# The transient factor of the last stage as 32x32 matmuls on diagonal tiles, for four images at once

## The chip, the cores and the metric

The kernel runs on one core of one Trainium2 chip. The metric is the device time of one execution in microseconds (us); the time before is the median of three runs, 3254.34 us (3249.64 to 3259.84).

## The reference

Sixteen images of sixteen channels with 256x256 points go through two layers. Both add to their input something computed from its group norm: a 3x3 circular convolution (written with FFTs in the reference), and then a Laplace layer with complex poles.

```python
    x = x + _L0_conv_ref(_gn(x), L0_conv_weight)
    x = x + _L1_conv_ref(_gn(x), L1_conv_ty, L1_conv_tx, ...)
```

Of the Laplace layer this is what matters here:

```python
        output_residue2 = jnp.einsum('bikpq,ikpq->bkpq', D, weights_residue)
        x1 = jnp.fft.ifft2(output_residue1, s=(Ny, Nx), axes=(-2, -1)).real
        E1 = jnp.exp(weights_pole1[..., None] * tyc)
        E2 = jnp.exp(weights_pole2[..., None] * txc)
        F = jnp.einsum('kbpq,bipz->kbiqz', output_residue2, E1)
        x2 = jnp.einsum('kbiqz,biqx->kizx', F, E2).real
        return x1 + x2 / Nx / Ny
```

`x1` is the steady part, an inverse transform. `x2` is the transient part: for one image k and one output channel i it is a product of three matrices, a table of exponentials along y, the residues of the image, and a table of exponentials along x.

## The kernel before

All arithmetic is float32. A float32 matmul is shown in the profile as two instructions of TensorE, so counts there are twice those of the code. The kernel has four stages:

- the convolution, from the start to about 760 us, with an order written out by hand; tables for later stages are computed beside it, among them the exponentials (`make_exps`, L384 to L426), which go to DRAM as `eD`: `eD[0]` along y, `eD[1]` along x;
- the forward transforms (L560 to L700), at whose end the residues of all images are put into the SBUF tile `o2`;
- the mixing over channels (L703 to L920), with an order written out by hand, which leaves its spectra in DRAM as `yD`;
- the last stage (L923 to L1006), which turns them back and adds the transient part. In it the framework's scheduler decides the order of the instructions on each engine from the program text, dependences and free buffers.

The last stage loops over 16 output channels `k`, and within one over four groups of four images (`b0`), so there are 64 groups and 256 images of one channel. For a channel, SP loads `yk` (its spectra, 4 MB, two buffers). For a group, SP loads `vl` (the layer's input, two buffers), and GpSimd computes four sums and differences `u` (L960) and scales a column (L963), two buffers. Then for each image:

1. `ps_h` (L974, TensorE): residues times the table along x, one matmul of 128x128 by 256 columns; ScalarE copies it to `hs` (L982).
2. `ps_p` (L985, TensorE): four matmuls of 128 columns from `u`, the inverse transform along x; ScalarE copies it to `pt` (L987).
3. `ps_f` (L990 and L991, TensorE): two matmuls from `pt` (the inverse transform along y) and two from `hs` with the table along y, all of 256 columns, in pairs that accumulate.
4. ScalarE copies one half of `ps_f` to `q` (L993); VectorE forms sum and difference `r` (L995, L996) and folds them out to the rows of `ol` (L997, L998).

After the four images VectorE adds `vl` to `ol` in one operation (L1001), and two stores to `out_y` are issued on ScalarE's queue (L1003). Each engine takes its instructions in the order of its own queue, and a DMA that is issued on ScalarE's queue stands in that order too.

The PSUM pools are `p_p` with three buffers, `p_h` with two and `p_f` with three, eight banks in all (L931 to L933). `pt`, `hs` and `q`, `r` have three buffers each, `ol` and `vl` two.

The matrix of residues that `ps_h` uses is 128x128, but only a quarter of it is not zero: rows 32kq to 32kq+31 (kq = 0 to 3 are four groups of channels or poles) belong to 16 columns of each of the two parts. The operations at L697 write it, four for each part, each with a mask column of `cols` (20 to 23):

```python
        for kq in range(4):
            nc.vector.tensor_scalar(
                o2[:, :, ro, 16 * kq : 16 * kq + 16], ps, cols[:, 20 + kq : 21 + kq], None, ALU.mult
            )
```

At its start the stage loads both tables, 2 MB each, in one tile `et` (L934 to L936), the constants `inv`, the first `yk` and the first two `vl`.

Of the kernel before, what the change touches and what calls it, by code (L numbers as in the profile page):

```python
# [9 lines left out]
FP = mybir.dt.float32  # L10
AF = mybir.ActivationFunctionType
ALU = mybir.AluOpType
AX = mybir.AxisListType
PSUM = bass.MemoryType.PSUM
DRAM = bass.MemoryType.DRAM

B = 16
C = 16
N = 256
P = 128  # L20
# [4 lines left out]
def conv_then_laplace_kernel(ctx: ExitStack, tc: tile.TileContext, a: dict, out: bass.AP):  # L25
# [15 lines left out]
    nc = tc.nc  # L41
    x = a["x"]

    cp = ctx.enter_context(tc.tile_pool(name="const", bufs=1))
    dp = ctx.enter_context(tc.tile_pool(name="scratch", bufs=1, space=DRAM))
# [6 lines left out]
    cols = const("cols", [P, 24])  # L52
    kmask = const("kmask", [P, C])
    trig = const("trig", [P, 2, P])
    o2 = cp.tile([P, B, 2, 64], FP, name="o2", tag="o2")

    vD = [dp.tile([2, P, C, N], FP, name=f"vD{b}", tag=f"vD{b}") for b in range(B)]
    aD = dp.tile([P, 2 * C, N * B], FP, name="aD", tag="aD")
    yD = dp.tile([P, 2 * C, 4, 2, 32 * B], FP, name="yD", tag="yD")
    cD = dp.tile([P, 4, 8, N], FP, name="cD", tag="cD")  # L60
    eD = dp.tile([2, P, C, 2, P], FP, name="eD", tag="eD")


    def omega(o, k, d):
# [28 lines left out]
    p1 = ExitStack()  # L93
# [290 lines left out]
    def make_exps(which):  # L384


        pl = sw.tile([P, C, 2], FP, name="s_pl", tag="s_pl")
        nc.sync.dma_start(out=pl, in_=a[f"pole_e{which + 1}"])
        t = sw.tile([P, N], FP, name="s_t", tag="s_t")
        nc.sync.dma_start(out=t, in_=a[("ty", "tx")[which]].to_broadcast([P, N]))  # L390
        sign, phase, turns = (cols[:, 2 + 3 * which + j : 3 + 3 * which + j] for j in range(3))
        pim = sw.tile([P, C], FP, name="s_pim", tag="s_pim")
        nc.vector.tensor_scalar(pim, pl[:, :, 1], sign, None, ALU.mult)
        yield
        for q in range(8):
            th = sw.tile([P, 2, N], FP, name="s_th", tag="s_th")
            rn = sw.tile([P, 2, N], FP, name="s_rn", tag="s_rn")
            ex = sw.tile([P, 2, N], FP, name="s_ex", tag="s_ex")
            for j in range(2):
                i = 2 * q + j  # L400
                nc.vector.tensor_scalar(th[:, j], t, pim[:, i : i + 1], None, ALU.mult)
                nc.scalar.activation(ex[:, j], t, AF.Exp, scale=pl[:, i, 0:1])
            nc.vector.tensor_scalar(rn, th, 1.0 / (2 * PI), turns, ALU.mult, ALU.add)
            magic = 1.5 * 2.0**23
            nc.vector.tensor_scalar(rn, rn, magic, None, ALU.add)
            nc.vector.tensor_scalar(rn, rn, magic, None, ALU.subtract)
            yield
            c1 = 6.28125
            c2 = float(np.float32(1.93500518798828125e-3))
            c3 = 2 * np.pi - c1 - c2  # L410
            for c in (c1, c2, c3):
                nc.vector.scalar_tensor_tensor(th, rn, -float(c), th, ALU.mult, ALU.add)
            nc.vector.tensor_scalar(th, th, phase, 3.1415925, ALU.add, ALU.min)
            nc.vector.tensor_scalar(th, th, -3.1415925, None, ALU.max)
            yield
            nc.scalar.activation(th, th, AF.Sin)
            yield
            nc.gpsimd.tensor_tensor(th, th, ex, ALU.mult)
            for op, eo in ((ALU.add, 0), (ALU.subtract, 1)):
                nc.gpsimd.tensor_tensor(  # L420
                    ex[:, :, eo * P : eo * P + P], th[:, :, 0:P], th[:, :, N - 1 : P - 1 : -1], op
                )
            yield
            nc.sync.dma_start(
                out=eD[which][:, 2 * q : 2 * q + 2].rearrange("p i e t -> p i (e t)"), in_=ex
            )  # L426

    def make_c():

# [105 lines left out]
    for g in range(24 * B + 3):  # L535
        conv(g)
        b, n = divmod(g, 24)
# [22 lines left out]
    p1 = ExitStack()  # L560
    kp = p1.enter_context(tc.tile_pool(name="b_const", bufs=1))
# [18 lines left out]
    m, n = cols[:, 16:17], cols[:, 17:18]  # L580
# [87 lines left out]
    for i in range(C):  # L668
        spec = ap.tile([P, 2, N, B], FP, name="spec", tag="spec")
        psd = pd.tile([P, B, 32], FP, name="psd", tag="psd")  # L670
        for b0 in range(0, B, 4):
            vf = fold(i, b0)
            t = lines(i, b0, vf)
            columns(i, b0, t, spec, psd)
        nc.scalar.dma_start(
            out=aD[:, 2 * i : 2 * i + 2].rearrange("p r n -> p (r n)"),
            in_=spec.rearrange("p r f b -> p (r f b)"),
# [14 lines left out]
    for ro in range(2):  # L692
        ps = pd.tile([P, B, 32], FP, name="psd", tag="psd")[:, :, 0:16]
        nc.tensor.matmul(ps, lhsT=jmat[:, 0], rhs=accs[:, ro], start=True, stop=False)
        nc.tensor.matmul(ps, lhsT=jmat[:, 2 - ro], rhs=accs[:, 1 - ro], start=False, stop=True)
        for kq in range(4):
            nc.vector.tensor_scalar(  # L697
                o2[:, :, ro, 16 * kq : 16 * kq + 16], ps, cols[:, 20 + kq : 21 + kq], None, ALU.mult
            )
    p1.close()  # L700
    ptab.close()

# [2 lines left out]
    kp = p2.enter_context(tc.tile_pool(name="m_const", bufs=1))  # L705
# [22 lines left out]
    sgn, nsgn, first = mcol[:, 6:7], mcol[:, 7:8], mcol[:, 8:9]  # L728
# [162 lines left out]
    for g in range(32):  # L891
# [3 lines left out]
        for n in range(0, 8, 2):  # L895
# [7 lines left out]
            for m in (n, n + 1):  # L903
                o, src = mix(m, sg, yt)
# [18 lines left out]
    p3 = ExitStack()  # L923
    kp = p3.enter_context(tc.tile_pool(name="e_const", bufs=1))
    yp = p3.enter_context(tc.tile_pool(name="yk", bufs=2))
    up = p3.enter_context(tc.tile_pool(name="ud", bufs=2))
    hp = p3.enter_context(tc.tile_pool(name="hl", bufs=3))
    qp = p3.enter_context(tc.tile_pool(name="ql", bufs=3))
    vp = p3.enter_context(tc.tile_pool(name="vl", bufs=2))
    op = p3.enter_context(tc.tile_pool(name="ol", bufs=2))  # L930
    pp = p3.enter_context(tc.tile_pool(name="p_p", bufs=3, space=PSUM))  # L931
    ph = p3.enter_context(tc.tile_pool(name="p_h", bufs=2, space=PSUM))
    pf = p3.enter_context(tc.tile_pool(name="p_f", bufs=3, space=PSUM))  # L933
    et = kp.tile([P, 2, C, 2, P], FP, name="et", tag="et")  # L934
    for j in range(2):
        nc.sync.dma_start(out=et[:, j], in_=eD[j])  # L936
    inv = kp.tile([P, 5, P], FP, name="inv", tag="inv")
    nc.sync.dma_start(out=inv, in_=a["inv"])
    cx, sx, nsx, cosY, sinY = (inv[:, j] for j in range(5))
# [1 line left out]
    for k in range(C):  # L941
        yk = yp.tile([P, 2, 2, 4, B, 32], FP, name="yk", tag="yk")
        nc.sync.dma_start(
            out=yk.rearrange("p r h c b j -> p (r h c b j)"),
            in_=yD[:, 2 * k : 2 * k + 2].rearrange("p r c h n -> p (r c h n)"),
        )
        for b0 in range(0, B, 4):
            bs = slice(b0, b0 + 4)
            vl = vp.tile([P, 2, 4, N], FP, name="vl", tag="vl")
            for j in range(4):  # L950
                nc.sync.dma_start(
                    out=vl[:, :, j], in_=vD[b0 + j][:, :, k, :].rearrange("h y x -> y h x")
# [15 lines left out]
                ALU.mult,  # L968
            )
            ol = op.tile([P, 2, 4, N], FP, name="ol", tag="ol")  # L970
            for j in range(4):
                b = b0 + j
                ps_h = ph.tile([P, N], FP, name="ps_h", tag="ps_h")
                nc.tensor.matmul(  # L974
                    ps_h,
                    lhsT=o2[:, b].rearrange("p r m -> p (r m)"),
                    rhs=et[:, 1, k].rearrange("p e t -> p (e t)"),
                    start=True,
                    stop=True,
                )  # L980
                hs = hp.tile([P, N], FP, name="hs", tag="hs")
                nc.scalar.copy(hs, ps_h)  # L982
                ps = pp.tile([P, 4, P], FP, name="ps_p", tag="ps_p")
                for n, (at, tab) in enumerate(((0, cx), (3, sx), (1, nsx), (2, cx))):
                    nc.tensor.matmul(ps[:, at], lhsT=u[:, j, n], rhs=tab, start=True, stop=True)  # L985
                pt = hp.tile([P, 2, N], FP, name="pt", tag="pt")
                nc.scalar.copy(pt, ps.rearrange("p (e n) x -> p e (n x)", e=2))  # L987
                ps = pf.tile([P, 2, N], FP, name="ps_f", tag="ps_f")
                for e, tab in ((0, cosY), (1, sinY)):
                    nc.tensor.matmul(ps[:, e], lhsT=tab, rhs=pt[:, e], start=True, stop=False)  # L990
                    nc.tensor.matmul(ps[:, e], lhsT=et[:, 0, k, e], rhs=hs, start=False, stop=True)  # L991
                q = qp.tile([P, N], FP, name="q", tag="q")
                nc.scalar.copy(q, ps[:, 1])  # L993
                r = qp.tile([P, 2, N], FP, name="r", tag="r")
                nc.vector.tensor_tensor(r[:, 0], ps[:, 0], q, ALU.add)  # L995
                nc.vector.tensor_tensor(r[:, 1], ps[:, 0], q, ALU.subtract)  # L996
                nc.vector.tensor_tensor(ol[:, :, j, 0:P], r[:, :, 0:P], r[:, :, P:N], ALU.add)  # L997
                nc.vector.tensor_tensor(  # L998
                    ol[:, :, j, N - 1 : P - 1 : -1], r[:, :, 0:P], r[:, :, P:N], ALU.subtract
                )  # L1000
            nc.vector.tensor_tensor(ol, ol, vl, ALU.add)  # L1001
            for h in range(2):
                nc.scalar.dma_start(  # L1003
                    out=out[k, bs, h].rearrange("b y x -> y b x"), in_=ol[:, h]
# [4 lines left out]
def _constants():  # L1009

    c = {}
    j = np.arange(N)
    p = np.arange(P)
# [14 lines left out]
    k = (j + P) % N - P  # L1028
# [3 lines left out]
    cols = np.zeros((P, 24))  # L1032
    even = p % 2 == 0
    cols[:, 0], cols[:, 1] = even, ~even
    first = p < 64
    cols[:, 2] = np.where(first, 1.0, -1.0)
    cols[:, 3], cols[:, 4] = np.where(first, np.pi / 2, 0), np.where(first, 0.25, 0)
    cols[:, 5] = 1.0
# [42 lines left out]
def _laid_out(x, L0_conv_weight, L1_conv_ty, L1_conv_tx, L1_conv_weights_pole1, L1_conv_weights_pole2, L1_conv_weights_residue):  # L1081
# [36 lines left out]
    z = np.broadcast_to(z[:, None, :, :, None], (2, 2, 4, 4, 2, 4, 8, 2))  # L1118
    g["pole2_k"] = z.reshape(P, 32, 2)

    e1 = p1.transpose(0, 2, 1, 3).reshape(64, C, 2)
    g["pole_e1"] = np.concatenate([e1, e1], 0)
    g["pole_e2"] = np.repeat(p2.transpose(0, 2, 1, 3).reshape(64, C, 2), 2, 0)
    return {n: np.ascontiguousarray(v) for n, v in g.items()}

# [16 lines left out]
```

## Time and profile before

| | us |
|---|---|
| median of the runs | 3254.34 |
| the profiled execution | 3263.39 |
| its span | 3261.5 |
| busy: PE / DVE / ACT / POOL over the span | 2731.3 / 1840.4 / 1342.9 / 942.9 |
| first ps_p of the last stage starts | 2449.69 |
| last pair of ps_f starts | 3251.21 |

The profile is of one execution. Its times are microseconds from the start of the span. PE is TensorE's matmuls, PEld its weight loads, DVE VectorE, ACT ScalarE, POOL GpSimd, SP the engine that issues most of the DMAs. In the groups by line, a row gives the line of the code, the engine, the operation, the tile written and those read, the shape and how often; then the busy time, the mean duration in ns, and the idle time of the engine just before such instructions with what ended it. These are rows of the last stage, from 2460 to 3250 us:

```profile
L990 PE MATMUL ps_f<-pt,inv 128*128 128x256 f32 x1009 | 313.6, 392 | 0.3
L991 PE MATMUL ps_f<-hs,et 128*128 128x256 f32 x1010 | 300.4, 379 | 0.0
L985 PE MATMUL ps_p<-inv,u 128*128 128x128 f32 x2024 | 286.8, 275 | 0.0
L998 DVE TENSOR_TENSOR ol<-r 128x256 f32<-128x256 f32 x253 | 195.5, 773 | 0.0
L974 PE MATMUL ps_h<-et,o 128*128 128x256 f32 x502 | 150.5, 382 | 3.1 <-ACT hs L982 3.1
L987 ACT COPY pt<-ps_p 128x512 f32<-128x512 f32 x253 | 149.8, 592 | 59.7 <-PE ps_p L985 51.9
L1001 DVE TENSOR_TENSOR ol<-ol,vl 128x2048 f32<-128x2048 f32 x63 | 144.4, 2292 | 2.1
L997 DVE TENSOR_TENSOR ol<-r 128x256 f32<-128x256 f32 x253 | 144.2, 570 | 42.2 <-DMA out_y<-ol 31.7 <-issue 2.3
L982 ACT COPY hs<-ps_h 128x256 f32<-128x256 f32 x251 | 97.1, 387 | 0.2
L993 ACT COPY q<-ps_f 128x256 f32<-128x256 f32 x252 | 93.8, 372 | 426.2 <-PE ps_f L991 382.3 <-DVE r L996 21.8 <-PE ps_p L985 15.7
```

Matmuls are pipelined: the mean duration of one reaches over the start of the next, so durations of a row add up to more than its busy time. A view in order of time gives the start, the length and the instruction, where several that follow each other are put together with their number.

### The profile page before, as it was taken

How to read it: one execution, taken by the hardware profiler on the slowest of the kernel's cores; microseconds unless marked ns; L12 is line 12 of the kernel's file. 1: busy time of each engine (PE TensorE's matmuls, PEld its weight loads, DVE VectorE, ACT ScalarE, POOL GpSimd, SP SyncE). 2: the span in 40 equal slices, each digit the busy share in tenths (PEclk: the TensorE clock that was granted, in tenths of full speed). 3: DMA queues.
4: the chain of work that ended last, by engine and by line, in shares of the span. 5: the costliest groups of instructions: out<-in, count | busy, mean ns of one | idle time of the engine just before them, and what ended most of it. 6: DMA issues, size and time to landing. Idle time of an engine off the chain costs nothing.

```text
span 3261.5 us, 104676 instructions
## 1 busy us (share of the span) xinstructions
PE 2731.3 (84%) x46188; PEld 1949.9 (60%) x46188; DVE 1840.4 (56%) x3584; ACT 1342.9 (41%) x2640; POOL 942.9 (29%) x753
## 2 busy tenths in 40 slices
PE   4878787796999999996676777777749999999998
PEld 1333333344777677764444545555438998999987
DVE  5555665565555555555343333334317888788787
ACT  2454676563444444442233333333313333333333
POOL 1111111002444455442111111111105444444442
PEclk9899898898999999997799899999979999999999
DMA  5455565665445555444265555655576776767764
GB/s 215 162 187 172 200 237 195 222 222 171 173 164 203 198 194 185 167 165 182 81 175 160 158 160 163 173 163 168 166 242 231 259 259 235 281 239 252 267 223 155
DMA packets 409158, 637.89 MB, mean 196 GB/s; under 512 B 30336, under 2 KB 364544, under 8 KB 400128
## 3 DMA queue, kind: packets, MB, share of 16 engines
q1 hardware_dynamic: 338816, 496.96, 46.8%
q10 hardware_dynamic: 69888, 134.23, 10.8%
q8 instruction: 364, 5.96, 0.7%
q14 instruction: 90, 0.74, 0.1%
HBM read 353.72 MB, written 277.35 MB: 193 GB/s over the span
## 4 chain that ended last, share of the span: by engine, by line
PE 47%; issue 10%; DVE 4%; DMA 4%; POOL 1%; ACT 1%; ACTq 0%; SPq 0%; DVEq 0%; POOLq 0%
PE ps_s L791 10%; PE ps_mix L839 9%; PE ps_f L990 5%; PE ps_f L991 5%; PE ps_p L985 5%; PE ps_x L648 3%; PE ps_y L608 3%; PE ps_y L616 3%; DMA out_y<-ol 3%; PE ps_h L974 2%; DVE ol L998 1%; DVE ol L1001 1%; DVE ol L997 1%; DVE sg L902 1%; DMA vl<-vD 1%
## 5 line engine op out<-in xcount | busy, mean ns | idle before, releaser
L223 PE MATMUL ps_conv<-xt,wc 32*32 32x512 f32 x12288 | 485.6, 646 | 29.9 <-ACT vt L241 20.8
L960 POOL TENSOR_TENSOR u<-yk 128x512 f32<-128x512 f32 x256 | 340.1, 1357 | 487.9 <-PE ps_p L985 411.3
L791 PE MATMUL ps_s<-ct,w 64*32 64x256 f32 (+1 forms) x8448 | 326.9, 415 | 132.6 <-issue 69.4
L839 PE MATMUL ps_mix<-abd,sg 128*32 128x64 f32 x16384 | 297.7, 229 | 134.9 <-issue 134.5
L839 PEld LDWEIGHTS ps_mix<-abd,sg 128*32 128x32 f32 x16384 | 262.8, 116 | 209.6 <-issue 199.1
L223 PEld LDWEIGHTS ps_conv<-xt,wc 32*32 32x32 f32 x12288 | 230.9, 107 | 235.9 <-issue 144.2
L902 DVE COPY sg<-ps_s 128x512 f32<-128x512 f32 x248 | 172.4, 699 | 342.8 <-PE ps_s L791 342.7
L624 ACT ACTIVATE t<-ps_y,vmr 128x768 f32<-128x768 f32 x256 | 229.7, 900 | 261.0 <-PE ps_y L616 235.9
L767 POOL TENSOR_TENSOR w<-v,mcol 128x2048 f32<-128x2048 f32 x33 | 118.8, 3599 | 717.2 <-DVE v L764 694.1
L608 PE MATMUL ps_y<-tabE,vf 128*128 128x256 f32 x1024 | 308.5, 383 | 17.1 <-DVE vf L595 13.2
L902 ACT COPY sg<-ps_s 128x512 f32<-128x512 f32 x248 | 168.5, 681 | 371.7 <-PE ps_s L791 371.6
L990 PE MATMUL ps_f<-pt,inv 128*128 128x256 f32 x1024 | 318.7, 393 | 0.3
L985 PEld LDWEIGHTS ps_p<-inv,u 128*128 128x128 f32 x2048 | 289.5, 192 | 33.7 <-POOL u L963 14.2
L616 PE MATMUL ps_y<-tabO,vf 128*128 128x256 f32 x1024 | 306.0, 381 | 2.0 <-DVE vf L598 2.0
L791 PEld LDWEIGHTS ps_s<-ct,w 64*32 64x32 f32 x8448 | 163.6, 115 | 239.4 <-issue 113.4
L991 PE MATMUL ps_f<-hs,et 128*128 128x256 f32 x1024 | 305.0, 379 | 0.0
L985 PE MATMUL ps_p<-inv,u 128*128 128x128 f32 x2048 | 291.2, 275 | 13.5 <-POOL u L963 13.5
L993 ACT COPY q<-ps_f 128x256 f32<-128x256 f32 x256 | 95.3, 372 | 432.7 <-PE ps_f L991 388.8
L590 POOL TENSOR_TENSOR s<-vy 128x1024 f32<-128x1024 f32 x64 | 151.7, 2371 | 419.9 <-issue 289.3
L648 PE MATMUL ps_x<-t,trig 128*128 128x512 f32 x512 | 247.3, 605 | 0.0
L253 DVE BATCH_NORM_STATS2 vst<-vt 128x6 f32<-128x512 f32 x128 | 88.0, 687 | 278.1 <-ACT vt L241 278.1
L608 PEld LDWEIGHTS ps_y<-tabE,vf 128*128 128x128 f32 x1024 | 193.9, 191 | 78.9 <-issue 43.8
(197 smaller groups left out, 4162.4 us busy)
## 6 DMA issues: line engine op xcount, KB each, us to landing
xt<-in_x SPq DMA_DIRECT2D x32, 2193.0 KB, 9.4
vD<-vt SPq DMA_DIRECT2D x256, 256.0 KB, 3.1
vy<-vD SPq DMA_DIRECT2D x256, 256.0 KB, 4.2
aD<-spec ACTq DMA_DIRECT2D x16, 4096.0 KB, 14.0
abd<-aD SPq DMA_DIRECT2D x512, 128.0 KB, 3.1
yD<-yt SPq DMA_DIRECT2D x256, 256.0 KB, 4.5
yk<-yD SPq DMA_DIRECT2D x16, 4096.0 KB, 14.2
vl<-vD SPq DMA_DIRECT2D x256, 256.0 KB, 6.3
```

What stands on the lines that cost most here:

```text
L223: nc.tensor.matmul(acc[r][32 * c : 32 * c + 32], lhsT=ready[b][0][rows, phase, tap], rhs=halves[b][u // 2][rows, q : q + 5 : 4, 2 - tap : ...
L608: nc.tensor.matmul(ps[:, xo, 0:N], lhsT=vf[:, xo, 0, j], rhs=tabE[:, 0 : i + 2 : i + 1], start=True, stop=False, skip_group_check=True,)
L616: nc.tensor.matmul(ps[:, xo, P : P + N], lhsT=vf[:, xo, 1, j], rhs=tabO[:, i : C + 1 : C - i], start=False, stop=True, skip_group_check=True,)
L624: nc.scalar.activation(t[:, :, j].rearrange("p e l n -> p e (l n)"), ps[:, :, 0:384], AF.Copy, scale=vmr[:, 0, b0 + j, i : i + 1],)
L648: nc.tensor.matmul(ps[xo], lhsT=tab, rhs=t[:, xo, j : j + 2, 0:3:2], start=True, stop=True)
L791: nc.tensor.matmul(ps[odd][32 * iq : 32 * iq + 32, ro, fy], lhsT=w[rows, iq, kk, ro], rhs=ct[rows, iq, kk, fy], start=True, stop=True,)
L839: nc.tensor.matmul(ps[32 * c : 32 * c + 32, j], lhsT=sg[:, 64 * c + 8 * n + j], rhs=abd[n // 2][:, :, c, 8 * (n % 2) + j], start=True, sto ...
L902: (nc.scalar.copy, nc.vector.tensor_copy)[j % 2](o, src)
L960: nc.gpsimd.tensor_tensor(u[:, :, j].rearrange("p b (c n) -> p c b n", c=4), in0, in1, o)
L985: nc.tensor.matmul(ps[:, at], lhsT=u[:, j, n], rhs=tab, start=True, stop=True)
L990: nc.tensor.matmul(ps[:, e], lhsT=tab, rhs=pt[:, e], start=True, stop=False)
L991: nc.tensor.matmul(ps[:, e], lhsT=et[:, 0, k, e], rhs=hs, start=False, stop=True)
```

## The change

The residues are kept without their zeros: `o2` has 16 columns for each part in place of 64, and one copy fills it where four masked operations did. The rows of the table along x are laid out so that each group of 32 rows of `o2` and of the table belong together. `ps_h` of one image becomes four matmuls of 32 rows, 32 columns of weights and 256 columns of data. That of rows kq writes the 32 partitions at 32((kq+j) % 4) of the bank of image j, so that the four matmuls of one image lie on four different row groups and column groups of the array, and those of the four images of a group take all 16 tiles. They are written for the four images together, ahead of the four copies to `hs`, which is now one tile of four.

The rows of `hs` of image j are thereby turned by j blocks of 32, and so the table along y has to be turned as well. `eD` becomes two tensors. The one along y is written twice, one copy behind the other, and for each channel SP loads four copies of it, each starting at another row, into a tile `ey` of two buffers (128 KB each). Only the table along x is loaded at the start of the stage.

The three PSUM pools become one of eight banks with one tag, which `ps_h`, `ps_p` and `ps_f` share.

```diff
-    o2 = cp.tile([P, B, 2, 64], FP, name="o2", tag="o2")
+    o2 = cp.tile([P, B, 2, 16], FP, name="o2", tag="o2")
...
-    eD = dp.tile([2, P, C, 2, P], FP, name="eD", tag="eD")
+    eD = [dp.tile([n, P, C, 2, P], FP, name=f"eD{n}", tag=f"eD{n}") for n in (2, 1)]
...
-            nc.sync.dma_start(
-                out=eD[which][:, 2 * q : 2 * q + 2].rearrange("p i e t -> p i (e t)"), in_=ex
-            )
+            for o in range(2 - which):
+                nc.sync.dma_start(
+                    out=eD[which][o, :, 2 * q : 2 * q + 2].rearrange("p i e t -> p i (e t)"),
+                    in_=ex,
+                )
...
-        for kq in range(4):
-            nc.vector.tensor_scalar(
-                o2[:, :, ro, 16 * kq : 16 * kq + 16], ps, cols[:, 20 + kq : 21 + kq], None, ALU.mult
-            )
+        nc.vector.tensor_copy(o2[:, :, ro], ps)
...
+    ep = p3.enter_context(tc.tile_pool(name="ey", bufs=2))
...
-    pp = p3.enter_context(tc.tile_pool(name="p_p", bufs=3, space=PSUM))
-    ph = p3.enter_context(tc.tile_pool(name="p_h", bufs=2, space=PSUM))
-    pf = p3.enter_context(tc.tile_pool(name="p_f", bufs=3, space=PSUM))
-    et = kp.tile([P, 2, C, 2, P], FP, name="et", tag="et")
-    for j in range(2):
-        nc.sync.dma_start(out=et[:, j], in_=eD[j])
+    pp = p3.enter_context(tc.tile_pool(name="p_inv", bufs=8, space=PSUM))
+    et = kp.tile([P, C, 2, P], FP, name="et", tag="et")
+    nc.sync.dma_start(out=et, in_=eD[1][0])
+    turned = eD[0].rearrange("o p k e t -> (o p) k e t")
...
+        ey = ep.tile([P, 4, 2, P], FP, name="ey", tag="ey")
+        for j in range(4):
+            nc.sync.dma_start(out=ey[:, j], in_=turned[P - 32 * j : 2 * P - 32 * j, k])
...
+            ps_h = [pp.tile([P, N], FP, name="ps_h", tag="ps") for _ in range(4)]
             for j in range(4):
-                b = b0 + j
-                ps_h = ph.tile([P, N], FP, name="ps_h", tag="ps_h")
-                nc.tensor.matmul(
-                    ps_h,
-                    lhsT=o2[:, b].rearrange("p r m -> p (r m)"),
-                    rhs=et[:, 1, k].rearrange("p e t -> p (e t)"),
-                    start=True,
-                    stop=True,
-                )
-                hs = hp.tile([P, N], FP, name="hs", tag="hs")
-                nc.scalar.copy(hs, ps_h)
-                ps = pp.tile([P, 4, P], FP, name="ps_p", tag="ps_p")
+                for kq in range(4):
+                    rows = slice(32 * kq, 32 * kq + 32)
+                    c = 32 * ((kq + j) % 4)
+                    nc.tensor.matmul(
+                        ps_h[j][c : c + 32],
+                        lhsT=o2[rows, b0 + j].rearrange("p r m -> p (r m)"),
+                        rhs=et[rows, k].rearrange("p e t -> p (e t)"),
+                        start=True,
+                        stop=True,
+                    )
+            hs = hp.tile([P, 4, N], FP, name="hs", tag="hs")
+            for j in range(4):
+                nc.scalar.copy(hs[:, j], ps_h[j])
+            for j in range(4):
+                ps = pp.tile([P, 4, P], FP, name="ps_p", tag="ps")
                 for n, (at, tab) in enumerate(((0, cx), (3, sx), (1, nsx), (2, cx))):
                     nc.tensor.matmul(ps[:, at], lhsT=u[:, j, n], rhs=tab, start=True, stop=True)
                 pt = hp.tile([P, 2, N], FP, name="pt", tag="pt")
                 nc.scalar.copy(pt, ps.rearrange("p (e n) x -> p e (n x)", e=2))
-                ps = pf.tile([P, 2, N], FP, name="ps_f", tag="ps_f")
+                ps = pp.tile([P, 2, N], FP, name="ps_f", tag="ps")
                 for e, tab in ((0, cosY), (1, sinY)):
                     nc.tensor.matmul(ps[:, e], lhsT=tab, rhs=pt[:, e], start=True, stop=False)
-                    nc.tensor.matmul(ps[:, e], lhsT=et[:, 0, k, e], rhs=hs, start=False, stop=True)
+                    nc.tensor.matmul(ps[:, e], lhsT=ey[:, j, e], rhs=hs[:, j], start=False, stop=True)
...
-    first = p < 64
+    first = p // 16 % 2 == 0
...
-    e1 = p1.transpose(0, 2, 1, 3).reshape(64, C, 2)
-    g["pole_e1"] = np.concatenate([e1, e1], 0)
+    e1 = p1.transpose(0, 2, 1, 3).reshape(4, 16, C, 2)
+    g["pole_e1"] = np.stack([e1, e1], 1).reshape(P, C, 2)
```

## The prediction

> **What bounds the kernel now.** I read the busy share and the clock in 40 slices first, then the last stage alone: its sums by engine, its groups by line, who waited for whom, and its order of time at three places. All edits but two lie in that stage, the last ten of the slices.
>
> ```profile
> PE   4878787796999999996676777777749999999998
> DVE  5555665565555555555343333334317888788787
> 2460.00:3250.00 790.00, 786.59 (x4545) 714.00 (x4544) 640.25 (x1073) 304.07 (x756) 358.14 (x310) 1.00 0.69 241
> ```
>
> The third line is the last stage (PE, PEld, DVE, ACT, POOL, granted clock, DMA share, GB/s). TensorE is busy 786.59 of 790 us at clock 1.00. Nothing else ends a wait there: VectorE has 81%, ScalarE 38%, and DMA 69%. From the first ps_p (2449.69) to the end of the last ps_f (3251.80) are 802.1 us for 64 groups of four images, so **12.53 us a group**, 3.13 an image.
>
> Why TensorE never waits is seen in the order of time:
>
> ```profile
> 2904.53 0.61 PE L985 MATMUL ps_p<-inv,u 128*128 128x128 f32 x4
> 2905.03 2.29 DVE L1001 TENSOR_TENSOR ol<-ol,vl 128x2048 f32<-128x2048 f32 x1
> 2905.41 0.61 PE L985 MATMUL ps_p<-inv,u 128*128 128x128 f32 x4
> 2905.87 0.70 PE L990 MATMUL ps_f<-pt,inv 128*128 128x256 f32 x2
> 2906.41 0.59 PE L991 MATMUL ps_f<-hs,et 128*128 128x256 f32 x2
> 2906.84 0.59 PE L990 MATMUL ps_f<-pt,inv 128*128 128x256 f32 x2
> 2907.27 0.59 PE L991 MATMUL ps_f<-hs,et 128*128 128x256 f32 x2
> 2907.36 1.02 ACTq L1003 DMA_DIRECT2D out_y<-ol  x2
> 2907.70 0.61 PE L985 MATMUL ps_p<-inv,u 128*128 128x128 f32 x4
> 2908.47 0.37 ACT L993 COPY q<-ps_f 128x256 f32<-128x256 f32 x1 [2.65 <-PE ps_p L985]
> ```
>
> While ScalarE copies the pt of one image, TensorE works on ps_p and ps_h of the next; ps_f of an image comes later. Two more things are to be seen: the sum ol+vl ends at 2907.32, the two stores are issued on ScalarE's queue right after it (1.02 us), and q, whose ps_f was done at about 2907.9, starts only behind them, at 2908.47. So a store that waits holds up ScalarE.
>
> What a turn costs without work ahead is seen where TensorE did run dry, at the start of the stage, and what follows a last ps_f at its end:
>
> ```profile
> 2460.12 1.95 PE L985 MATMUL ps_p<-inv,u 128*128 128x128 f32 x16
> 2461.26 0.59 ACT L987 COPY pt<-ps_p 128x512 f32<-128x512 f32 x1 [0.57 <-PE ps_p L985]
> 2461.90 0.70 PE L990 MATMUL ps_f<-pt,inv 128*128 128x256 f32 x2
> ...
> 3251.21 0.59 PE L991 MATMUL ps_f<-hs,et 128*128 128x256 f32 x2
> 3251.89 0.37 ACT L993 COPY q<-ps_f 128x256 f32<-128x256 f32 x1 [1.40 <-PE ps_f L991]
> 3252.29 0.42 DVE L995 TENSOR_TENSOR r<-ps_f,q 128x256 f32<-128x256 f32 x1 [0.22 <-ACT q L993]
> 3253.88 2.29 DVE L1001 TENSOR_TENSOR ol<-ol,vl 128x2048 f32<-128x2048 f32 x1
> 3256.20 0.94 ACTq L1003 DMA_DIRECT2D out_y<-ol  x2
> ```
>
> **What the Trainium skill says.** "TensorE: Matmul & The Clock Gate", Part 3, The mechanism: matmuls start and end strictly in order, and only weight loads are pulled ahead. The trace agrees where TensorE ran dry: nothing behind the ps_f of 2461.90 went ahead of it while it waited for its pt. The same page, Part 3, Measured speedup: 16 tiles of 32x32 give 10.6 times one tile. Here the convolution (L223, 32x32 tiles) issues 239 matmuls in 8.11 us of busy time at clock 1.00 (500 to 510 us), 34 ns each, where one of 512 columns alone takes 430 ns (ps_x, L648): 12.7 times, so it packs at least as well. The same page, Part 1: the clock is gated by activity in windows of about 3.4 us. Here a gap of 1.97 us before 2221.38 was followed by 64 matmuls of L791 in 3.40 us against 1.96 elsewhere (mean clock 0.72 in 2220 to 2225), while one of 2.63 us before 2247.37 cost nothing. "SBUF — State Buffer", SBUF: two separate sides: VectorE operations with two SBUF inputs and GpSimd lock each other out for a whole instruction. Here L998 takes 0.42 us, and 1.49 beside GpSimd's L960.
>
> **The change part by part.**
>
> *ps_h.* Two full matmuls an image go, 8 a group, at 0.216 us (pairs of the same size start 0.43 us apart: 2906.41, 2906.84, 2907.27): 1.73 us. In their place stand 32 instructions of 32x32 tiles and 256 columns (each matmul counts twice, as before). Their form is not in this trace. Between the 17 ns each of L839 (128 in 2.17 us, 64 columns) and the 34 ns of L223 (512 columns) that is 0.54 to 1.09 us; if only the four diagonal tiles of one image ran at once it would be 1.73. I take 0.8 with the two changes of tile shape. By itself: 0.93 us a group saved, 59 us in all.
>
> *The order.* The built program of the changed kernel puts TensorE's work of all 64 groups in this order: ps_h of four images, then ps_p, ps_f, ps_p, ps_f, ps_p, ps_f, ps_p, ps_f, each ps_f for the image of the ps_p just ahead of it. The before program had one or two ps_p and a ps_h between them. So each ps_f now waits for a pt whose ps_p has just ended, and behind it in the queue stands everything that TensorE has. One turn, from the first matmul of ps_f: 1.83 us to the next ps_p (2905.87 to 2907.70); 1.14 from there to the start of pt (2460.12 to 2461.26; again 2900.92 to 2902.06); 0.59 for pt; 0.05 to ps_f. **3.61 us** an image, of which TensorE works 2.72. q doesn't lengthen it: it is ready 2.05 after the first matmul of ps_f, done at 2.42, and pt starts at 2.97.
>
> *Between groups.* ScalarE's order is four hs, pt of image 0, the two stores of the group before, q of image 0, pt of image 1. Count from the first matmul of image 3's ps_f. ps_h starts at 1.83, ps_p at 2.63, pt at 3.77, ps_f of image 0 at **4.41**. The four hs fit beside it: back to back such copies start 0.27 us apart (2908.47 and 2908.74 in the trace), so 2.5 to 3.6. On VectorE, q is done at 2.42, r starts at 2.45, and ol+vl follows 1.59 later (3252.29 to 3253.88) with nobody beside it. But GpSimd begins the u of a later group when image 3's ps_p ends, at about -0.6, and works 5.4 to 5.9 us (2647.33 to 2653.6). So image 3's L998, and in part its L997, wait for it: 1.07 (1.49-0.42) and 0.3 to 0.7. ol+vl starts at about 5.45, the stores are issued 2.32 later at 7.75, and hold ScalarE for 1.0. q of image 0, ready at 6.46, starts at 8.8, pt of image 1 is behind it at 9.1, done at 9.7, and its ps_f starts at 9.75: **5.34** in place of 3.61. Without the lock it would be 3.7 to 4.
>
> The group is 4.41+5.34+3.61+3.61 = 16.97 us, with TensorE idle 2.6 us in one piece. The clock may fall there: bounds are nothing, and every group paying a window at half speed, some 1.7 us. I take 0.5, so **17.5 us**. Against 12.53 that is 4.97 x 64 = +318 us.
>
> *Transfers.* At the start 2.1 MB of table fewer stand ahead of yk, and 0.5 to 1 MB of ey are new. At the 410 GB/s of 2425 to 2440, when DMA is saturated and GpSimd waits for yk, that is -3 to -4 us; I take -4, bounds -8 and 0. Later 8 MB of ey come in at 128 KB a piece, on SP between vl loads that are issued a group or two early; with a longer group the traffic falls below today's 241 GB/s. Nothing; if its cover were gone, the landing of one, about 6 us, sixteen times, some 100 us. Eight more writes of the table in the convolution, on SP, beside 256 vD stores: nothing, at worst 8 issues of 0.33 us.
>
> *o2.* Six of eight VectorE operations of 0.4 us go. The first three lie on the path (TensorE waits for the single psd buffer, 1519.77 to 1521.48), the others beside the loads of the next stage: -1, bounds -2.5 and 0.
>
> The evictions stay: four hs of 256 columns a group. The shared PSUM slots bring no wait of their own: they free after r of images long done, but for the third ps_p, which needs r of image 3, ready by 3.3.
>
> Sum: 318-4-1 = +313 us. The profiled execution took 3263.39 (span 3261.5), 9 above the median; on the median, 3254.34+313 = **3567 us**.
>
> **The rivals.**
> *No block by the stores* (16%): each image costs its wait for pt, but ScalarE is not held. For it: the stores may be issued early if ol+vl ends sooner; against it 2908.47. 4x3.61+0.8 = 15.24 a group, +173-5: 3422.
> *The clock* (7%): with TensorE working 2.72x4+0.8 = 11.7 of 17 us (69%, as much as in the stage of L839, whose clock was 0.89), the grant falls to 0.75. 3.9 more on 17: 20.9 a group, +531: 3785.
> *Faster* (3%): the wait for pt is covered after all, and the stage stays bound by the sum of TensorE: 12.53-0.93 = 11.6 a group, so -59-5: 3190. It decides once some other TensorE work of about 0.9 us stands between ps_p and its ps_f; the built order has none, and by order in the queue none can slip in.
> *No effect* (2%): saving and waits cancel, or the order is not run as built; 3254.
>
> **How the numbers follow.** Forecast 72%, its own range 3470 to 3650 (16.1 to 18.8 a group). Range 3410 to 3650: it takes in the case without the block, and leaves out the lower clock and the faster side. What this measurement can tell from no change is about 0.3%, 10 us. Slower 0.95 (the forecast and the first two rivals), same 0.02, faster 0.03.
>
> **What would show it.** In the profile after: TensorE at 65 to 75% in the last stage, with idle before the first ps_f of an image put down to pt, 0.7 to 0.9 us each; q of image 0 starting after the two stores; the second ol operation near 1.5 us for image 3; ps_h as 32 instructions within 1 us. A last stage over 85% busy, or ps_p of the next image between a ps_p and its ps_f, would make the prediction wrong.

## The result and the profile after

The changed kernel takes 3537.43 us (median of 4 runs, 3533.34 to 3541.62); the kernel before 3252.30 (median of 4 runs, 3249.64 to 3259.84). The ratio is 1.0873, with a 95% interval of 1.0848 to 1.0898: slower by 285 us. The profiled execution took 3541.62, its span is 3539.8. Against the profiled execution of before, whose span is 3261.5, that is +278.3.

In the busy shares of the 40 slices the last stage begins near slice 28, as before:

```profile
PE   4877877879999999947777777774777777777776
PEclk9999988989999999969999999997999999999999
```

TensorE has fallen from 9 to 7 tenths there, and the granted clock has not fallen with it. The sums by engine of the last stage (PE, PEld, DVE, ACT, POOL, granted clock, DMA share, GB/s) say the same in numbers:

```profile
2480.00:3530.00 1050.00, 779.70 (x5884) 634.05 (x5882) 692.41 (x1045) 302.31 (x735) 354.28 (x300) 0.98 0.54 185
```

779.70 of 1050 us are 74%, where it was 786.59 of 790. No other engine has taken its place: VectorE has 66%, the DMA has less to do per microsecond than before. So the stage waits. For what, the view of waits of the same stretch says (engine and tile that waited, what it waited for, sum in us, times, longest):

```profile
PE ps_f L998 <- ACT pt L995: 270.3, 246, 3.0
ACT q L1001 <- issue: 232.8, 55, 4.5
```

All of TensorE's idle time, 1050 - 779.70 = 270.3 us, stands in the first line: it waits for pt, 246 times, which is once for each image in the stretch. The second line is ScalarE's: 55 times, in nearly every group, it stands still for up to 4.5 us, for which the profile names no other engine ("issue"), and then makes q.

The order of time over one group shows both (TensorE's first pair of ps_f of images 3, 0, 1 and 2, and what stands between them):

```profile
3000.33 5.50 POOL L962 TENSOR_TENSOR u<-yk 128x512 f32<-128x512 f32 x4 [10.74 <-PE ps_p L993]
...
3000.97 0.70 PE L998 MATMUL ps_f<-pt,inv 128*128 128x256 f32 x2 [0.73 <-ACT pt L995]
...
3002.90 0.71 PE L980 MATMUL ps_h<-et,o 32*32 32x256 f32 x32
...
3003.54 1.16 PE L993 MATMUL ps_p<-inv,u 128*128 128x128 f32 x8
...
3004.63 1.48 DVE L1006 TENSOR_TENSOR ol<-r 128x256 f32<-128x256 f32 x1
3004.79 0.59 ACT L995 COPY pt<-ps_p 128x512 f32<-128x512 f32 x1
...
3005.43 0.70 PE L998 MATMUL ps_f<-pt,inv 128*128 128x256 f32 x2 [0.73 <-ACT pt L995]
...
3006.14 2.29 DVE L1009 TENSOR_TENSOR ol<-ol,vl 128x2048 f32<-128x2048 f32 x1
...
3008.47 1.02 ACTq L1011 DMA_DIRECT2D out_y<-ol  x2
...
3009.86 0.37 ACT L1001 COPY q<-ps_f 128x256 f32<-128x256 f32 x1 [4.48 <-issue]
3010.13 0.59 ACT L995 COPY pt<-ps_p 128x512 f32<-128x512 f32 x1
...
3010.77 0.70 PE L998 MATMUL ps_f<-pt,inv 128*128 128x256 f32 x2 [2.46 <-ACT pt L995]
...
3014.39 0.70 PE L998 MATMUL ps_f<-pt,inv 128*128 128x256 f32 x2 [0.73 <-ACT pt L995]
```

From image 3 to image 0 are 4.46 us, from 0 to 1 5.34, from 1 to 2 3.62, and 3.61 to the next image 3 at 3018.0. The 5.34 is read upwards: ps_f of image 1 waits for pt (3010.13), pt stands behind q (3009.86), q behind the two stores (3008.47), the stores behind ol+vl (3006.14), and that behind an L1006 of 1.48 us which ran beside GpSimd's u.

Over the 59 groups between 2480 and 3480 whose turns can be read, the four turns are in the mean 4.46, 5.11, 3.95 and 3.62, together 17.14 us. The third isn't even: it is 3.62 in 46 groups, 5.0 to 5.3 in 12 and 3.89 in one. One of the twelve, in the order of time:

```profile
2698.84 1.22 PE L998 MATMUL ps_f<-pt,inv 128*128 128x256 f32 x2 [2.18 <-ACT pt L995]
...
2699.85 1.06 PE L999 MATMUL ps_f<-hs,ey 128*128 128x256 f32 x2
```

and the sums by engine of just this stretch, with the clock third from the end:

```profile
2698.84:2702.30 3.46, 3.46 (x9) 2.81 (x9) 1.01 (x3) 0.00 (x0) 0.00 (x0) 0.52 1.08 374
```

Pairs that otherwise take 0.59 take 1.06: after the gap behind the stores the array ran 3.46 us at half clock. So the clock does cost something, in one group of five.

Where the 278.3 us of the two profiles lie, by marks that both have:

| stretch | change, us |
|---|---|
| to the last start of the convolution (760.8, now 767.7) | +6.9 |
| from there to the first ps_mix (1590.3, now 1597.9) | +0.7 |
| first to last start of ps_mix (2412.5, now 2404.3) | -15.8 |
| last ps_mix to first ps_p (37.1, now 31.0) | -6.1 |
| first ps_p to the end of the last ps_f (802.1, now 1094.65) | +292.6 |

The last row is 17.10 us a group of four images in place of 12.53. The rows above it are small, and partly no work of the change: in the profiles of the eight kernels that follow, which all have the same mixing stage, the last ps_mix starts anywhere from 2399 to 2427.

### The profile page after: what moved, and what is told of

The parts are those of the page before. It is cut to its first block, busy times and chain, and to the rows that moved or that the text cites. A ratio compares the mean times of both kernels' runs of the same rounds, so it can differ in the third digit from the quotient of the medians.

```text
span 3539.8 us, 107683 instructions
## 1 busy us (share of the span) xinstructions
PE 2735.9 (77%) x47724; PEld 1879.1 (53%) x47724; DVE 1911.6 (54%) x3578; ACT 1350.6 (38%) x2640; POOL 950.8 (27%) x753
## 4 chain that ended last, share of the span: by engine, by line
PE 44%; issue 11%; DVE 9%; DMA 5%; ACT 4%; ACTq 2%; POOL 1%; SPq 0%; DVEq 0%; POOLq 0%
PE ps_s L790 9%; PE ps_mix L838 8%; PE ps_f L998 6%; PE ps_x L650 5%; PE ps_f L999 4%; PE ps_y L610 4%; PE ps_y L618 4%; DVE ol L1009 4%; PE ps_p L993 3%; ACT pt L995 3%; DVE ol L1006 2%; DMA vl<-vD 2%; DMA out_y<-ol 1%; ACTq L1011 1%; PE psd L639 1%
## 5 line engine op out<-in xcount | busy, mean ns | idle before, releaser
L998 PE MATMUL ps_f<-pt,inv 128*128 128x256 f32 x1024 | 343.1, 418 | 280.4 <-ACT pt L995 280.4
L962 POOL TENSOR_TENSOR u<-yk 128x512 f32<-128x512 f32 x256 | 350.6, 1398 | 761.0 <-PE ps_p L993 689.5
L998 PEld LDWEIGHTS ps_f<-pt,inv 128*128 128x128 f32 x1024 | 179.1, 195 | 344.2 <-ACT pt L995 329.4
L1003 DVE TENSOR_TENSOR r<-ps_f,q 128x256 f32<-128x256 f32 x256 | 108.8, 425 | 397.4 <-ACT q L1001 397.4
L999 PE MATMUL ps_f<-hs,ey 128*128 128x256 f32 x1024 | 314.5, 390 | 0.0
L993 PEld LDWEIGHTS ps_p<-inv,u 128*128 128x128 f32 x2048 | 267.0, 193 | 53.8 <-issue 25.9
L993 PE MATMUL ps_p<-inv,u 128*128 128x128 f32 x2048 | 278.8, 279 | 15.9 <-POOL u L965 15.9
```

What stands on the lines that cost most here:

```text
L962: nc.gpsimd.tensor_tensor(u[:, :, j].rearrange("p b (c n) -> p c b n", c=4), in0, in1, o)
L999: nc.tensor.matmul(ps[:, e], lhsT=ey[:, j, e], rhs=hs[:, j], start=False, stop=True)
```

## The experiments

The theory: the time is lost because ps_f stands right behind the ps_p that it needs by way of pt, and because the stores on ScalarE's queue hold up the next q and pt once a group. Its rivals: that the tiles of 32x32, the table in turned copies or the lower clock cost the time themselves. And one thing was open: which part of the change makes the order. Each ratio below is to the kernel before as it was timed along with that run (3255.98 us with the pools, the look-ahead and the stores of the changed kernel, 3253.25 with the others), so a difference of medians from different sets is good to some 4 us.

**Only the pool.** The kernel before, with nothing but its three PSUM pools put into one:

```diff
-    pp = p3.enter_context(tc.tile_pool(name="p_p", bufs=3, space=PSUM))
-    ph = p3.enter_context(tc.tile_pool(name="p_h", bufs=2, space=PSUM))
-    pf = p3.enter_context(tc.tile_pool(name="p_f", bufs=3, space=PSUM))
+    pp = p3.enter_context(tc.tile_pool(name="p_inv", bufs=8, space=PSUM))
...
-                ps_h = ph.tile([P, N], FP, name="ps_h", tag="ps_h")
+                ps_h = pp.tile([P, N], FP, name="ps_h", tag="ps")
...
-                ps = pp.tile([P, 4, P], FP, name="ps_p", tag="ps_p")
+                ps = pp.tile([P, 4, P], FP, name="ps_p", tag="ps")
...
-                ps = pf.tile([P, 2, N], FP, name="ps_f", tag="ps_f")
+                ps = pp.tile([P, 2, N], FP, name="ps_f", tag="ps")
```

> The kernel before with one edit: its three PSUM pools of the last stage (3, 2 and 3 banks) are replaced by one pool of eight banks with one tag. The table, ps_h as a full matmul and the loads stay as before. Theory A (the order: with one shared pool the scheduler keeps the program text's order, so each ps_f stands right behind its ps_p on TensorE and waits for pt): one image 4.04 us (1.83 ps_f, 0.43 ps_h, 1.14, 0.59 and 0.05), with the stores' block of some 1.4 us once a group about 17.5 us a group, 3570 us in all (3500 to 3620), although nothing of the 32x32 tiles is in it. Theory B (the cost of the new pieces: 32x32 tiles, change of tile shape, loads of ey): 3252, no change.

It took 3581.54 us (3577.2 to 3592.26), 1.1008 of before (1.0972 to 1.1044). Without one 32x32 tile and without a turned table it is slower than the changed kernel. Its order of time (before's operations, now at lines 972 to 1001):

```profile
2905.35 0.70 PE L988 MATMUL ps_f<-pt,inv 128*128 128x256 f32 x2 [1.92 <-ACT pt L985]
...
2907.18 0.59 PE L972 MATMUL ps_h<-et,o 128*128 128x256 f32 x2
...
2907.61 1.05 PE L983 MATMUL ps_p<-inv,u 128*128 128x128 f32 x8
...
2909.39 0.70 PE L988 MATMUL ps_f<-pt,inv 128*128 128x256 f32 x2 [0.73 <-ACT pt L985]
```

The built order is that of the program's text, image by image: ps_h, ps_p, ps_f, with the same wait of 0.73 us for pt. A turn is 4.04 us, 0.43 more than in the changed kernel, which is the one pair of ps_h. So the shared pool alone takes the work ahead away, and the rest of the change, put on top of it, wins time: 3581.54 to 3537.43.

**The pools apart again.** The changed kernel with three pools, of four, two and two banks, and its text unmoved:

```diff
-    pp = p3.enter_context(tc.tile_pool(name="p_inv", bufs=8, space=PSUM))
+    ph = p3.enter_context(tc.tile_pool(name="p_h", bufs=4, space=PSUM))
+    pp = p3.enter_context(tc.tile_pool(name="p_p", bufs=2, space=PSUM))
+    pf = p3.enter_context(tc.tile_pool(name="p_f", bufs=2, space=PSUM))
```

> The changed kernel with separate PSUM pools again: four banks for ps_h, two for ps_p, two for ps_f. Nothing in the program text is moved. Theory A: the scheduler looks ahead again (two ps_p, then two ps_f, with ps_h of the next group between), and the waits of 0.9 us an image go; with only two ps_f banks and the stores on ScalarE about 12.4 us a group: 3245 us (3190 to 3270). Theory B: stays above 3450.

3301.94 us (3296.98 to 3312.68), ratio 1.0146 (1.0105 to 1.0187). Two ps_p now stand ahead of two ps_f again (x16 is the ps_p of two images), and 235 us of the 285 are gone:

```profile
2901.64 1.95 PE L995 MATMUL ps_p<-inv,u 128*128 128x128 f32 x16
...
2904.11 0.69 PE L1000 MATMUL ps_f<-pt,inv 128*128 128x256 f32 x2
```

The expected 3245 is missed, and so is its range. One reason is in its waits from 2480 to 3100 us, of which this is the longest line on ps_f:

```profile
PE ps_f L1000 <- DVE r L1006: 40.6, 31, 3.3
```

With two banks left for ps_f, TensorE waits for VectorE to have read the one before last. That was the price of giving four banks to ps_h. The expectation named the two banks, but its 12.4 us a group was too little: the stage took 13.28 (2444.12 to 3294.27). The stores are still on ScalarE's queue as well.

**The look-ahead by the text alone.** The changed kernel, shared pool kept, with ps_p and pt of the next image written ahead of ps_f:

```diff
+            first(0)
             for j in range(4):
-                ps = pp.tile([P, 4, P], FP, name="ps_p", tag="ps")
-                for n, (at, tab) in enumerate(((0, cx), (3, sx), (1, nsx), (2, cx))):
-                    nc.tensor.matmul(ps[:, at], lhsT=u[:, j, n], rhs=tab, start=True, stop=True)
-                pt = hp.tile([P, 2, N], FP, name="pt", tag="pt")
-                nc.scalar.copy(pt, ps.rearrange("p (e n) x -> p e (n x)", e=2))
+                if j < 3:
+                    first(j + 1)
+                pt = pts[j]
```

Here `first(j)` holds the five lines taken out.

> The changed kernel with one edit of the program text: ps_p and pt of image j+1 are written ahead of ps_f of image j. The shared PSUM pool, the 32x32 tiles, ey and the stores on ScalarE stay. Theory A: ps_f never follows its own ps_p any more, so TensorE has 0.9 us of other work there; the group falls from 17.1 to 11.5 if TensorE is the bound, or to 12.1 to 12.5 if the stores still hold up pt of image 2: 3190 to 3260 us. Theory B (cost of the tiles, their change of shape and ey): stays above 3450.

3276.65 us (median of 7 runs, 3264.87 to 3281.59), ratio 1.006 (1.0038 to 1.0082). 261 us of the 285 come back with the same tiles, the same tables and the same pool: the order is the cause of most of the loss. It stays above the expected range, and above before. Its waits from 2480 to 3100 us:

```profile
ACT q L1010 <- DMA out_y<-ol: 70.2, 12, 6.7
...
PE ps_f L1007 <- ACT pt L997: 50.0, 39, 3.0
```

What is left of TensorE's waits for pt comes where ScalarE is held by a store: each of the 39 ends within 4.1 us after a store was issued there, and with the stores on SP (next) the view has no such wait.

**The stores elsewhere.** The changed kernel with its stores issued on SP; then the same one-word edit on the version with the text in look-ahead order, and on the kernel before:

```diff
-                nc.scalar.dma_start(
+                nc.sync.dma_start(
                     out=out[k, bs, h]
```

> The changed kernel with its two stores of a group issued on SP's queue in place of ScalarE's. Theory A (order, and the stores hold up q of image 0 and pt of image 1): the turn of 5.34 us falls to 3.61, the group from 17.1 to 15.4, 3537-110 = 3425 us (3405 to 3445). Rival (q waits anyway, for VectorE or for ps_f): 3537. Second rival (stores on SP hold up the loads of vl and yk behind them): above 3450.

> The run with ps_p of image j+1 ahead of ps_f of image j, and the two stores issued on SP in place of ScalarE. Theory: what keeps that run (3277 us, 12.75 us a group) from TensorE's own sum of 11.5 us is pt of image 2 behind the stores on ScalarE; without them TensorE is the bound, 11.7 us a group, 3277-67 = 3210 us (3190 to 3235). Rival (VectorE, 83% busy there, or the DMAs are the next bound): 3240 to 3277.

> The kernel before, with its two stores of a group issued on SP in place of ScalarE and nothing else changed. TensorE is busy in 786.6 of 790 us of its last stage, so there is nothing to win but the gaps between 12.2 us of matmuls and 12.53 us a group: 3235 to 3260. If the gain of the run with look-ahead and stores on SP came from the stores alone, this one would show it too (3210).

On the changed kernel: 3439.52 us (3433.38 to 3446.95), ratio 1.0568 (1.0533 to 1.0602), so 98 us less. Its order of time over the stores:

```profile
2902.69 0.70 PE L998 MATMUL ps_f<-pt,inv 128*128 128x256 f32 x2 [0.73 <-ACT pt L995]
...
2903.39 2.29 DVE L1009 TENSOR_TENSOR ol<-ol,vl 128x2048 f32<-128x2048 f32 x1
...
2904.76 0.37 ACT L1001 COPY q<-ps_f 128x256 f32<-128x256 f32 x1 [2.13 <-PE ps_f L999]
...
2905.67 0.58 ACT L995 COPY pt<-ps_p 128x512 f32<-128x512 f32 x1 [0.53 <-PE ps_p L993]
2905.72 0.95 SPq L1011 DMA_DIRECT2D out_y<-ol  x2
...
2906.30 0.70 PE L998 MATMUL ps_f<-pt,inv 128*128 128x256 f32 x2 [0.73 <-ACT pt L995]
```

pt of image 1 no longer waits for ol+vl: the turn over the stores is 3.61 us, as the other two, and the slow turns behind it are gone (3.63 in the mean). That is 5.11 + 3.95 - 3.61 - 3.63 = 1.82 us a group, 116 us; 98 were measured.

With both, the look-ahead and the stores on SP: 3192.08 us (3186.58 to 3200.77), ratio 0.9801 (0.9777 to 0.9826), faster than before by about 2%. On the kernel before the stores alone bring nothing: 3260.93 (median of 18 runs), 1.0018 (1.0006 to 1.003), 1 us above the expected range. There TensorE was full already, and it stays so (sums by engine, columns as above; first the version with both, then before with the stores on SP):

```profile
2480.00:3100.00 620.00, 611.16 (x5129) 528.65 (x5128) 583.04 (x911) 266.15 (x641) 319.02 (x267) 1.00 0.83 285
2460.00:3250.00 790.00, 790.00 (x4489) 715.13 (x4488) 671.14 (x1060) 306.96 (x748) 365.64 (x309) 1.00 0.70 240
```

A full TensorE need not mean a shorter stage: with the stores on SP the built order of before is a little different (once a group it had the ps_f of two images in a row, now never), 4489 matmul instructions start in these 790 us where there were 4545, and the last stage of the profile takes 811.2 us in place of 802.1.

So the gain of the version with both isn't one of the stores alone. At 61 us it is near the 59 that the shorter ps_h was put at.

**GpSimd's lock.** The changed kernel with u made in the first group of a channel only; the sums of the other three groups are left out, and their images are made from the u of the first:

```diff
-            u = up.tile([P, 4, 4, P], FP, name="u", tag="ud")
+            if b0 == 0:
+                u = up.tile([P, 4, 4, P], FP, name="u", tag="ud")
...
```

> The changed kernel, with u computed by GpSimd for the first group of a channel only and read by all four: the sums and differences of the other three groups are left out. TensorE's order and the waits for pt stay. Theory (GpSimd's u keeps ol of image 3 back, and through ol+vl and the stores also q of image 0 and pt of image 1): in 48 of 64 groups ol+vl starts 1.5 us sooner and the turn of 5.34 us falls to some 3.9: 3537-67 = 3470 us (3450 to 3490). Rival (the block is the stores' own issue time): 3537.

3502.4 us (3498.31 to 3508.13), ratio 1.0747 (1.0721 to 1.0774): 35 us less, half of what was expected. The order of time in two groups without a u near them (lines are one higher than in the changed kernel):

```profile
2928.44 0.70 PE L999 MATMUL ps_f<-pt,inv 128*128 128x256 f32 x2 [0.73 <-ACT pt L996]
...
2930.37 3.08 ACTq L1012 DMA_DIRECT2D out_y<-ol  x2
...
2933.55 0.37 ACT L1002 COPY q<-ps_f 128x256 f32<-128x256 f32 x1 [5.16 <-DMA out_y<-ol]
...
2947.42 0.70 PE L999 MATMUL ps_f<-pt,inv 128*128 128x256 f32 x2 [0.73 <-ACT pt L996]
...
2949.35 1.02 ACTq L1012 DMA_DIRECT2D out_y<-ol  x2
2951.38 0.70 PE L999 MATMUL ps_f<-pt,inv 128*128 128x256 f32 x2 [1.07 <-ACT pt L996]
```

Without the lock the turn over the stores is 2951.38 - 2947.42 = 3.96 us. It is 3.9 to 4.0 in 33 of the 61 groups; 15, about as many as there are groups in which u is still made, have 5.0 to 5.2. But in 8 it is 5.4 to 6.2: in the one shown the two stores are 3.08 us in the queue, not 1.02, while SP's loads of the next channel's ey are under way (2930.37). So the lock's size shows where nothing else delays the stores, and in about one group of eight something else does. Over the four turns the group falls from 17.14 to 16.39 us, 48 us in all. The last stage itself bears this out (1094.65 us in the one profile, 1048.8 in the other: 46); the two profiles differ by 13 us in the other direction ahead of it, where the programs are the same (last ps_mix at 2417.4 and 2404.4).

**A version that beats both.** The change's tiles and tables and its shared pool, with the last stage's order written by hand: ps_f two images behind ps_p, ps_h of the next group between, the stores on SP.

```diff
+    p3.enter_context(tc.manual_schedule())
...
+    LAG = 2
+    for i in range(16 * C + LAG):
+        g, j = divmod(i, 4)
+        if g < 4 * C:
...
+            for n, (at, tab) in enumerate(((0, cx), (3, sx), (1, nsx), (2, cx))):
+                nc.tensor.matmul(ps[:, at], lhsT=us[g][:, j, n], rhs=tab, start=True, stop=True)
...
+        if j == 3 and g + 1 < 4 * C:
+            hss[g + 1], copies = exps(g + 1)
+        if i < LAG:
+            continue
+        g, j = divmod(i - LAG, 4)
...
+        for e, tab in ((0, cosY), (1, sinY)):
+            nc.tensor.matmul(ps[:, e], lhsT=tab, rhs=pt[:, e], start=True, stop=False)
+            nc.tensor.matmul(ps[:, e], lhsT=ey[:, j, e], rhs=hs[:, j], start=False, stop=True)
...
```

> The changed kernel's 32x32 tiles, ey and shared PSUM pool, with the order of the last stage written by hand: ps_f two images behind ps_p, ps_h of the next four between, u of a group made one group ahead, stores on SP. Theory: TensorE never waits, 4x(1.73+0.89)+0.95 = 11.43 us a group and some 0.1 of gaps, 1.0 below the 12.53 of before: 3252-64 = 3188 us (3175 to 3215). Rival (VectorE, kept from SBUF by GpSimd for some 1.1 us at a time, can't keep up with 11.5 us a group): 3215 to 3260.

3184.53 us (3180.68 to 3199.19), ratio 0.9784 (0.9755 to 0.9814): the lowest median of all, 69 us below before. Its interval overlaps with that of the version with the look-ahead in the text and the stores on SP; which of the two is faster these runs don't tell. The sums by engine, and then the order of time over the end of a group:

```profile
2480.00:3100.00 620.00, 620.00 (x5214) 546.34 (x5213) 576.76 (x927) 263.29 (x652) 356.54 (x273) 1.00 0.81 285
```

```profile
2903.42 0.60 PE L1035 MATMUL ps_f<-pt,inv 128*128 128x256 f32 x2
2903.85 0.59 PE L1036 MATMUL ps_f<-hs,ey 128*128 128x256 f32 x2
...
2906.04 0.60 PE L1035 MATMUL ps_f<-pt,inv 128*128 128x256 f32 x2
...
2908.75 0.79 PE L992 MATMUL ps_h<-et,o 32*32 32x256 f32 x32
...
2909.47 0.70 PE L1035 MATMUL ps_f<-pt,inv 128*128 128x256 f32 x2
```

TensorE is full again. An image takes 2.62 us (2903.42 to 2906.04), the one with ps_h 3.43, so ps_h of four images costs 0.81 us where its eight full matmuls had cost 1.73. The group is 3x2.62 + 3.43 = 11.29 us against 12.53. Of these 1.24 us ps_h is 0.92. The other 0.32 come with the order; part of it is seen at the first pair of ps_f, behind which the next pair starts 0.43 us later here (2903.42 to 2903.85) and 0.54 in the kernel before (2905.87 to 2906.41). What before's full ps_h would take in an order written by hand wasn't tried, so not all of the 69 us belong to the tiles.

## Why the prediction was right

The forecast, 3567 us, was 30 us (0.8%) too high, inside its own range, and the mechanism is the one that it gave. Point by point:

| step | put at, us | measured, us |
|---|---|---|
| ps_h of a group | 0.8 | 0.85 (4.46 - 3.61); 0.81 in the hand-ordered version |
| turn of one image | 3.61 | 3.62 |
| image 3 to image 0 | 4.41 | 4.46 |
| image 0 to image 1 | 5.34 | 5.11 in the mean |
| clock, a group | 0.5 | 0.33 |
| group | 17.5 | 17.14 by its turns, 17.10 over the stage |
| last stage | +318 | +292.6 |
| start of the stage | -4 | -6.1 |
| o2 | -1 | +0.7 over a stretch that holds more than it |

*The order* was read from the built program, and the chip ran it so. That the turn could be priced to 0.01 us came from pieces that the trace of before held. One of them was misread. The prediction says that TensorE ran dry at 2460.12 and that the ps_f of 2461.90 waited for its pt; but the sixteen ps_p there are those of two images, and the second eight fill TensorE to 2461.90. From the first ps_p to pt (1.14) and the length of pt (0.59) can be read there all the same. The last step, 0.05 from the end of pt to ps_f, is right by luck: at 2461.90 the end of pt and the end of the queue ahead fell together. After the change it can be read without doubt (pt ends at 3005.38, ps_f starts at 3005.43), and there nothing behind the ps_f goes ahead while it waits.

*The block by the stores* is there, and the rival without it falls: with the stores on SP that case, which the prediction put at 3422, was made to happen, and took 3439.52. Its size was a little too large. ol+vl was put 5.45 us behind the first ps_f of image 3 and comes 5.17 behind it (3000.97 to 3006.14). In most groups the rest follows as worked out, and the turn is about 5.07; the group shown above is one where q came later behind the stores (1.39 us after their start, 1.12 at 2696.81). That it has exactly the 5.34 of the prediction is luck: ol+vl came 0.28 sooner than reckoned, and q 0.34 later behind the stores (1.39 for 1.05).

*The lock's share*, put at 1.3 to 1.6 us by "without the lock it would be 3.7 to 4", is 1.1: about 5.07 in most groups with it, 3.96 in most without.

*The clock* was the term with the widest bounds, and it was neither nothing nor the rival's 3.9 us a group. The 3.95 of the third turn are 0.33 more than 3.62: 12 groups of 59 pay 1.6 us. The Trainium skill, "TensorE: Matmul & The Clock Gate", Part 1, says that the window of the gate is about 3.4 us long and free-running, that is, not tied to when the work starts. The trace agrees with both: the slow stretch is 3.46 us, and gaps of nearly the same length (2.18 us before 2698.84, 2.46 before 3010.77) cost it once and not the other time. More of it is in the trace's record of the granted clock: the stage has twelve slow stretches of 3.41 us, and their starts lie whole multiples of 3.41 us apart, most often 25 or 30 of them (85.3 or 102.4 us). So it seems to be the gap's place in the window that decides; no run moved it alone. The faster rival needed some other TensorE work between ps_p and its ps_f, and none was there; the two versions that put it there and freed ScalarE ended at 3192.08 and 3184.53, beside the 3190 that this rival had been put at.

The overestimate is made of the group's length (25 us: 15 from the block and 11 from the clock, 4 against them from the other turns, the rest rounding) and of the stretches ahead of the stage, which changed by -14.3 in these two profiles where -5 had been put (start of the stage and o2). Most of that is the mixing stage, which the change doesn't touch: its matmuls took 822 us in this one profile of before, 806 after, and 804 to 817 in the other eight. The convolution's +6.9 may be the eight added writes of the table, which the prediction put at nothing: the three kernels with before's convolution end it at 759.9 to 765.8, the seven with the change's at 765.0 to 778.7. They weren't tried alone, so this stays open. From profile to profile the sum is 35 us too high, from median to median 30: the profiled execution of before lay 9 us above the first median, that of after 4 above its own.

What the prediction didn't have is the reason for the order. It wrote that the shared PSUM slots bring no wait of their own, which holds: in the waits of after TensorE waits for nothing but pt. But putting the pools together is what lets the built order fall back to that of the text; it costs 325 us by itself, more than the whole change.

## What to carry to other kernels

A wait that was hidden by work ahead has a price that the old trace can show: read the pieces of the chain there, add them up once, multiply the sum by its repetitions, and compare it with the work that the change saves (here some 0.9 us a group saved, 5.5 lost). When tiles are moved into one pool, look at the built order of each engine before anything else, for the order may have rested on the pools being apart; if it is lost, write it into the text or by hand. And an engine whose copies feed the bottleneck shouldn't issue stores that wait for another engine: here that was worth nothing while TensorE had work ahead, 98 us when it had none, and 85 when the order was mended.

## What was not expected of the hardware

A gap on TensorE in every period of 17 us, of 2.2 to 2.5 us in most, left the mean clock at 0.98: only 12 of 59 were followed by a stretch of about 3.46 us at half speed. Where the gaps were shorter, 162 of at most 1.0 us in 620 (the changed kernel with its stores on SP), the clock was 1.00.

Thirty-two matmul instructions of 32x32 tiles with 256 columns start within 0.64 us (3002.90 to 3003.54), 20 ns each. This is near the lower of the two bounds, 17 and 34 ns, that other tile shapes had given. ps_h has 0.81 to 0.85 us in all, so about 0.2 us are left for the two changes of tile shape in a group; that is a difference of these figures, and the changes weren't tried alone.

Two stores issued one right behind the other on ScalarE took 1.02 us in the groups shown of the changed kernel, but 3.08 where SP's loads of the next tables were under way (2930.37 in the version with fewer u). Why the second has to wait there wasn't settled.
